# Eight loads of x moved from ahead of the last table's reads to among them

## The chip, the cores and the metric

The kernel runs on one core of a Trainium2 chip. The metric is device time in microseconds (us). Three runs of the kernel before took 4207.98, 4208.53 and 4208.92 us; the median is 4208.53 us. One more execution was profiled.

A core has five engines with a queue of their own each: TensorE (PE in the rows; PEld is its weight load), VectorE (DVE), ScalarE (ACT), GpSimd (POOL) and SyncE (SP, which here only issues DMA transfers). Every queue is worked through in order. The 16 DMA engines of the core move the data; an engine waits for data or for another engine through semaphores.

## The reference, cut to what matters

A graph layer over 12,500 atoms with 128 features and 412,500 edges, sorted by destination atom:

```
h    = maximum(layernorm(x), 0) @ W_in2f
Wij  = (softplus(f_ij @ W_f1 + b_f1) - log 2) @ W_f2 + b_f2
Wij  = Wij * rcut_ij[:, None]
x_ij = h[idx_j] * Wij                                   # 412500 x 128, a message per edge
agg  = segment_sum(x_ij, idx_i, num_segments=12500)
out  = (softplus(agg @ W_o1 + b_o1) - log 2) @ W_o2 + b_o2
return x + out
```

In the call, `idx_i` is `src` and `idx_j` is `dst`. All is float32. The last line is the part that matters here: each output row is x, plus the output bias b_o2 (into which the constant log 2 is folded), plus a product.

## The kernel before, in words

**Main loop.** The edges are worked in 806 chunks of 512. For each chunk the kernel computes the edge filter, picks the rows of h by a matmul with a comparison mask, multiplies both to 512 messages (`message`, tile `o`), and scatters them with four indirect DMAs from GpSimd's queue (`scatter`, line 873) into a table of slots in device memory. There are seven tables (`SEGS`), one after the other. While chunks run, the table that is complete is read back and summed per atom (`Collect`). The last four groups of 2048 edges go to the seventh table, `slots6`, and this one can be read only after the last scatter into it has landed.

**A table's sum.** `Collect` cuts a table into units. `load(u)` issues a read of unit u from SP into a tile `m` of seven buffers (line 919). `compare(u)` makes a 0/1 matrix `to` (five buffers) that says which of the 128 atoms of a block each slot belongs to: on VectorE in one instruction (line 932), on GpSimd in one instruction per block (line 938). `add(u)` multiplies the two on TensorE into PSUM (line 953), and `keep` adds the result to `agg` on VectorE (line 987). The seventh table has 27 units: 22 with four blocks, five with two blocks of two tiles each.

**Loads of x.** The output is made in 25 quads of four blocks, 512 atoms each (the last has two pieces, of 128 and 84 rows). Every quad needs its x rows (256 KB a quad), loaded by `x_load` from SP (line 428), and the bias added by `x_bias` (line 433). Eight early quads are loaded during the main loop, with VectorE adding the bias. The other 17, the late ones, have their tiles in buffers that the main loop has given up: `late_homes` gives eight quads in the buffers of `rel` (named `xr`), four in those of `f` (`xf`), two in those of `hg` (`xh`), three in those of `o` (`xm`). The generator `x_ahead` loads and biases them in order. For the late quads it is run in one go, after the main loop and ahead of the final table's first read, with the bias on GpSimd, where these additions stand behind the last scatters.

**The tail.** After it comes a loop over the 27 units of the final table, written out by hand: five reads are issued ahead and two comparisons made, then at each unit u the read of unit u + 5 is issued, unit u + 2 is compared (on GpSimd where u is odd and over 6, else on VectorE), unit u is summed, and the quad that is complete takes one stage further (`stages`): the first output matmul (line 443), three ScalarE functions (446, 411, 412), VectorE's line 449, the second output matmul (453), VectorE's addition to x (457), and the store from SP (460). The stages of five successive quads are in flight at once. So the order on SP is: late loads of x, five reads, and then a read and a store in turn; on GpSimd: scatters, biases, comparisons. SP's DMAs use eight completion semaphores in turn, so a DMA is not issued before the one eight places ahead of it has landed.

The loop of the tail is this:

```
for u in range(len(last.units)):
    last.load(u + 5)
    if u + 2 < len(last.units):
        last.compare(u + 2, nc.gpsimd if u > 6 and u % 2 else nc.vector)
    done = last.done
    last.done = []
    last.add(u)
    if done:
        ...
        stages(q)
        q += 1
```

Of the kernel before, what the change touches and what calls it, by code (L numbers as in the profile page):

```python
# [21 lines left out]
QT = CH // P  # L22
# [18 lines left out]
def ceil_div(a, b):  # L41
    return -(-a // b)
# [3 lines left out]
def gnn_kernel(  # L46
# [20 lines left out]
    nc = tc.nc  # L67
# [5 lines left out]
    NTILE = ceil_div(N, P)  # L73
# [47 lines left out]
    def sbuf(name, shape, dtype=F32):  # L121
        return const.tile(shape, dtype, name=name)

    def spread(t, n):
        return t[:, None, :].to_broadcast([t.shape[0], n, P])
# [21 lines left out]
    bf2, bo2 = (sbuf(n, [P, P]) for n in ("bf2", "bo2"))  # L147
# [87 lines left out]
    def relative(k):  # L235
        n = parts_c[k][1]
        d0 = ln.tile([P, 1], F32, name="d0")
        nc.vector.tensor_copy(d0[:n, :], d0_i[k][:n, :])
        nc.vector.tensor_scalar(rel[:n, k, :], dc[k][:n, :], d0[:n, :], None, op0=ALU.subtract)
# [174 lines left out]
    def x_pieces(t0, n):  # L414

        n0 = t0 * P
        full = min(n, N // P - t0)
        rest = N - n0 - full * P if full < n else 0
        pieces = []
        if full:  # L420
            pieces.append((P, slice(0, full), slice(n0, n0 + full * P)))
        if rest:
            pieces.append((rest, slice(full, n), slice(n0 + full * P, N)))
        return pieces

    def x_load(xo, pieces):
        for p, cs, rows in pieces:
            nc.sync.dma_start(xo[:p, cs, :], x[rows, :].rearrange("(c p) f -> p c f", p=p))

    def x_bias(xo, pieces, engine=nc.vector, b=bo2):  # L430
        for p, cs, rows in pieces:
            xi = xo[:p, cs, :]
            engine.tensor_add(xi, xi, spread(b[:p, :], xi.shape[1]))
# [111 lines left out]
    with tc.tile_pool(name="edge", bufs=2) as edge, tc.tile_pool(  # L545
# [491 lines left out]
        def group(j):  # L1037
            if j not in groups and j < NG:
                groups[j] = Group(j)
# [110 lines left out]
        t0, i = 8, 0  # L1150
        while i < len(segs):
# [5 lines left out]
            t0, i = due[j], j + 1  # L1157
# [20 lines left out]
        i, k = 0, todo[0][0]  # L1178
# [12 lines left out]
        def x_ahead(homes, engine, b):  # L1191

            pending = []
            for q, xo in homes:
                n = min(QT, NTILE - q * QT)
                pieces = x_pieces(q * QT, n)
                x_load(xo, pieces)
                xs[q] = xo
                pending.append((xo, pieces))
                yield  # L1200
                yield
                if len(pending) > 2:
                    x_bias(*pending.pop(0), engine, b)
            for w in pending:
                yield
                x_bias(*w, engine, b)

        def as_quad(t):
            return t.rearrange("p (c f) -> p c f", f=P)

        xs = {}
        NX = 8

        def early_homes():
            for q in range(NX):
                if q < 6:
                    yield q, ln.tile([P, QT, P], F32, name="xo", tag=("xb", "xT", "left")[q // 2],
                                     bufs=2)
                else:
                    t = ln.tile([P, QT, 3, P], BF16, name="xo", tag="hb", bufs=2)  # L1220
                    yield q, as_quad(t.rearrange("p c k f -> p (c k f)")[:, :2 * CH].bitcast(F32))

        def late_homes():
            for q in range(NX, NX + 12, 2):
                if q < NX + 8:
                    t = edge.tile([P, NCHUNK, CH], BF16, name="xr", tag="rel", bufs=4)
                    t = t.rearrange("p c e -> p (c e)").bitcast(F32)
                else:
                    t = edge.tile([P, NB, CH], F32, name="xf", tag="f")
                    t = t.rearrange("p b e -> p (b e)")  # L1230
                for i in range(2):
                    yield q + i, as_quad(t[:, i * CH:(i + 1) * CH])
            for q in range(NX + 12, NX + 14):
                yield q, quad.tile([P, QT, P], F32, name="xh", tag="hg")
            for q in range(NX + 14, NQ):
                t = quad.tile([P, QT, RW], F32, name="xm", tag="o", bufs=BACK)
                yield q, t[:, :, :P]
# [34 lines left out]
        with tc.manual_schedule():  # L1272
            constants()
            nc.scalar.activation(count_ps, places, AF.Copy)
            h = [make_h(q, psum) for q in range(2)]
            next(h[0])
            next(h[0])
            relative(0)
            shift(0)
            group(0)  # L1280
            early[1] = load_x(1)
            next(h[0])
            groups[0].edges()
            next(h[0])
            part("hidden", 0, hidden)
            groups[0].blocks(0)
            made["blocks"] = 0
            next(h[0])
            groups[0].half_log(0)
            next(h[0])  # L1290
            part("rows", 3, rows)
            biases(psum)
            bs[0] = groups[0].bias(0)
            groups[0].half_log(1)
            made["log"] = 0
            ready = ranks(0)
            next(ready)
            groups[0].starts()
            groups[0].half_end(0)
            part("window", 0, window)  # L1300
            vs[0] = groups[0].value(0, bs.pop(0))
            next(ready, None)
            made["rank"] = 0
            groups[0].half_end(1)
            made["end"] = 0
            group(1)
            aside = side()
            x_early = x_ahead(early_homes(), nc.vector, bo2_ps)
            x_late = x_ahead(late_homes(), nc.gpsimd, bo2)
            for k in range(-3, max(NCH, max(units) + 1)):  # L1310
                for seg, d in zeros.get(k, ()):
                    seg.clears.append(nc.sync.dma_start(*d).ins.name)
                now = units.get(k, ())
                for c, u in now:
                    if u == 0:
                        for i in range(AHEAD):
                            c.load(i)
                if k == NCH:
                    kept["rest"] = True
                step(k, now)  # L1320

                if k >= 0:
                    for m in h:
                        next(m, None)
                if k > NEXT - 3:
                    next(aside, None)
                if k >= XK:
                    next(x_early, None)
            summed[0].add(summed[1])
            for c in owed:  # L1330
                c.keep()
            owed.clear()
            worst = state.tile([1, 1], F32, name="worst")
            nc.vector.tensor_reduce(worst, bad, axis=mybir.AxisListType.X, op=ALU.max)
            nc.vector.tensor_copy(flag, worst)
            for _ in x_early:
                pass
            for _ in x_late:
                pass


            last = collects[-1]
            z = psum.tile([P, 2, CH], F32, name="z_out", tag="z")
            outs = []
            for q in range(NQ):
                n = min(QT, NTILE - q * QT)
                sT = kept["agg"][:, q * QT:q * QT + n, :].rearrange("p c f -> p (c f)")
                outs.append(finish(q * QT, n, sT, quad, psum, z[:, q % 2, :], xs[q]))

            def stages(q):  # L1350
                for d in (1, 2, 3, 4, 5):
                    if 0 <= q - d < NQ:
                        next(outs[q - d], None)

            for u in range(5):
                last.load(u)
            last.compare(0)
            last.compare(1)
            q = 0
            for u in range(len(last.units)):  # L1360
                last.load(u + 5)
                if u + 2 < len(last.units):
                    last.compare(u + 2, nc.gpsimd if u > 6 and u % 2 else nc.vector)
                done = last.done
# [3 lines that stand above are left out]
                    now, last.done = last.done, done  # L1368
                    last.keep()
                    last.done = now  # L1370
                    stages(q)
                    q += 1
            last.keep()
            owed.clear()
            for q in range(q, NQ + 5):
                stages(q)
# [56 lines left out]
```

## Time and profile before

| | us |
|---|---|
| median of three runs | 4208.53 |
| lowest, highest | 4207.98, 4208.92 |
| profiled execution | 4207.59 |
| its span, first to last instruction | 4205.9 |
| TensorE busy | 3305.9 (79%) |
| VectorE busy | 3134.5 (75%) |
| ScalarE busy | 2774.6 (66%) |
| GpSimd busy | 3137.6 (75%) |
| last scatter on GpSimd begins | 4108.09 |
| first read of the final table issued | 4119.62 |
| its comparison begins | 4123.84 |
| last addition to x on VectorE begins | 4198.90 |

Shares of busy time are means over the whole span, of which the stretch at the change is the last 3%. The rows that matter are those of the last 110 us. A row of a time line gives the start in us from the start of the span, the duration, the engine (SPq is SP's queue), the line, the operation with its tiles, how many instructions are merged in the row, and in brackets how long the engine idled before and what ended it. A float32 matmul is counted as two instructions, so one unit of four blocks shows as x8. A DMA share over 1 means that transfers overlapped on an engine.

### The profile page before, as it was taken

What the parts mean: (1) busy time and instruction counts of PE and PEld (TensorE: products, weight loads), DVE (VectorE), ACT (ScalarE), POOL (GpSimd) and SP (SyncE); (2) the same over time, 40 slices, a digit from 0 to 9 for tenths busy, and PEclk for the clock granted to TensorE, in tenths of its full rate; (3) what the DMA queues carried; (4) which work ended last, traced back from release to release, by engine and by line L of the source; (5) the groups of instructions that cost most, each with busy time, mean ns of one, the idle gap of its engine ahead of it and who ended that gap; (6) DMA issues with size and microseconds to landing.
All of it is one profiled execution on the core that took longest, in us unless ns stands there. A gap on an engine that the chain in (4) does not pass through costs nothing. (4 is left out here: it accounts for less than half of the span.)

```text
span 4205.9 us, 68388 instructions
## 1 busy us (share of the span) xinstructions
PE 3305.9 (79%) x21594; PEld 2564.3 (61%) x21594; DVE 3134.5 (75%) x7192; ACT 2774.6 (66%) x5494; POOL 3137.6 (75%) x3298
## 2 busy tenths in 40 slices
PE   6777667676676666678888888988888888888887
PEld 4555445444444444457776776767777767667786
DVE  7887666666555555668877887888888888888986
ACT  6887676667666666666666666766666666666624
POOL 5777777777777777777777777777777777777774
PEclk8877776667766667679999998999999999999999
DMA  5776655655444354467778777778777977787776
GB/s 173 215 231 210 193 171 178 188 158 177 142 127 132 110 169 152 139 198 235 230 227 278 226 220 214 229 227 278 232 229 205 297 230 209 235 243 213 218 231 192
DMA packets 494767, 858.10 MB, mean 204 GB/s; under 512 B 141018, under 2 KB 276558, under 8 KB 494398
## 3 DMA queue, kind: packets, MB, share of 16 engines
q1 hardware_dynamic: 390798, 640.38, 52.1%
q0 software_dynamic: 103168, 213.15, 15.0%
q8 instruction: 174, 2.85, 0.3%
q14 instruction: 195, 1.60, 0.1%
q10 hardware_dynamic: 432, 0.13, 0.0%
HBM read 457.62 MB, written 395.69 MB: 203 GB/s over the span
## 5 line engine op out<-in xcount | busy, mean ns | idle before, releaser
L873 POOL DMA_INDIRECT slots<-o,slot x3224 | 3093.3, 959 | 1011.8 <-issue 720.4
L856 ACT ACTIVATE hg<-picked,rcut 128x128 f32<-128x128 f32 x3224 | 909.6, 364 | 409.5 <-PE picked L846 396.2
L834 PEld LDWEIGHTS v<-wf,r 128*128 128x128 f32 x6448 | 997.4, 233 | 252.4 <-issue 128.1
L834 PE MATMUL v<-wf,r 128*128 128x128 f32 x6448 | 1075.4, 321 | 24.2 <-ACT v L826 11.7
L953 PEld LDWEIGHTS acc<-to,m 128*128 128x128 f32 x5660 | 723.4, 205 | 213.4 <-DVE agg L987 87.6
L826 ACT ACTIVATE v<-bf 128x512 f32<-128x512 f32 x806 | 484.8, 601 | 535.2 <-DVE o L864 516.0
L710 PE MATMUL z<-f,wf 20*128 20x512 f32 x1612 | 564.5, 783 | 346.2 <-DVE r L742 343.9
L953 PE MATMUL acc<-to,m 128*128 128x128 f32 x5660 | 768.1, 293 | 71.0 <-DVE agg L987 51.1
L863 DVE COPY o<-place 128x4 f32<-128x4 f32 x806 | 151.8, 188 | 678.7 <-DMA slots<-o,slot 677.6
L932 DVE TENSOR_TENSOR to<-numbers,m 128x640 f32<-128x640 f32 (+3 forms) x793 | 629.7, 824 | 29.4 <-DMA m<-slots 19.7
L846 PE MATMUL picked<-near,at 126*128 126x128 bf16 x3224 | 363.7, 243 | 329.2 <-DVE o L864 322.8
L864 DVE TENSOR_TENSOR o<-v,hg 128x512 f32<-128x512 f32 x806 | 552.3, 685 | 80.3 <-PE v L834 75.1
L742 DVE SCALAR_TENSOR_TENSOR r<-z,nbf,a 128x1024 f32<-128x1024 f32 x402 | 512.8, 1276 | 81.3 <-ACT a L722 80.6
L846 PEld LDWEIGHTS <-at 126*128 126x128 bf16 x3224 | 290.5, 111 | 380.4 <-issue 310.7
L747 DVE TENSOR_TENSOR inb<-numbers,blk 128x392 f16<-128x392 f32 x806 | 446.1, 554 | 96.0 <-PE numbers L953 95.7
L719 ACT ACTIVATE a<-z,bf 128x1024 f32<-128x1024 f32 x402 | 442.4, 1101 | 113.8 <-PE z L710 113.5
L722 ACT ACTIVATE a<-a,half 128x1024 f32<-128x1024 f32 x402 | 461.6, 1148 | 13.1
L710 PEld LDWEIGHTS z<-f,wf 20*128 20x128 f32 x1612 | 142.3, 215 | 522.1 <-DVE r L742 493.2
L771 DVE TENSOR_REDUCE top<-free 128x4 f32<-128x392 f32 x806 | 446.1, 553 | 13.0 <-PE free L766 12.5
L720 ACT ACTIVATE a<-a 128x1024 f32<-128x1024 f32 x402 | 424.9, 1057 | 12.7
L953 PEld LDWEIGHTS numbers<-to,m 128*128 128x128 f32 x2492 | 326.7, 211 | 156.3 <-DVE to L932 145.2
L953 PE MATMUL numbers<-to,m 128*128 128x128 f32 x2492 | 354.9, 301 | 69.7 <-DVE to L932 68.8
(126 smaller groups left out, 1984.8 us busy)
## 6 DMA issues: line engine op xcount, KB each, us to landing
m<-slots SPq DMA_DIRECT2D x307, 387.0 KB
rel<-rel_d SPq DMA_DIRECT2D x202, 504.0 KB
m<-slots SPq DMA_DIRECT2D x278, 322.5 KB
f<-in_f_t SPq DMA_DIRECT2D x101, 512.0 KB
slots<-o,slot POOLq DMA_INDIRECT x3224
m<-slots SPq DMA_DIRECT2D x193, 258.0 KB
slots<-zero SPq DMA_DIRECT2D x96, 387.0 KB
slots<-zero SPq DMA_DIRECT2D x58, 516.0 KB
```

The source lines that it names most:

```text
L710: mm = nc.tensor.matmul(z[:, k, :], wf1[rows, :], self.f[rows, :], start=True, stop=True)
L722: nc.scalar.activation(a, a, AF.Ln, bias=half, scale=0.5)
L742: nc.vector.scalar_tensor_tensor(r, z, nbf1, a, op0=ALU.max, op1=ALU.add)
L747: nc.vector.tensor_tensor(inb, count_ps[:, None, :NBLK].to_broadcast([P, QT, NBLK]), self.blk[:, c * QT:(c + 1) * QT, None].to_broadcast([ ...
L826: nc.scalar.activation(v, spread(bf12, QT), AF.Copy)
L834: mm = nc.tensor.matmul(v[:, i, :], r[:, i * P:(i + 1) * P], wf2, start=False, stop=True, skip_group_check=True)
L846: mm = nc.tensor.matmul(ps[:, i, :], at[:, i * P:(i + 1) * P], near, start=i == 0, stop=i == QT - 1, skip_group_check=True)
L856: nc.scalar.activation(hg[:, i, :], ps[:, i, :], AF.Copy, scale=self.rcut[:, j:j + 1])
L864: nc.vector.tensor_mul(o[:, :, :P], v, hg)
L873: put = nc.gpsimd.indirect_dma_start(out=views[j % VIEWS], out_offset=bass.IndirectOffsetOnAxis(ap=self.slot[:, j:j + 1], axis=0), in_=o[: ...
L932: nc.vector.tensor_tensor(to[:, :n, :], count_ps[:, None, :].to_broadcast([P, n, P]), m[:, :n, P:].to_broadcast([P, n, P]), op=ALU.is_equal)
L953: nc.tensor.matmul(self.acc[b // few][:, i, :], m[:, j, :P], to[:, j, :], start=t == 0, stop=t == self.seg.tiles(b) - 1)
```

## The change

The 17 late quads are no longer loaded and biased in one go. `NOW` = 9 of them are loaded there, and their bias is added on GpSimd as before. The other eight (three of `xf`, two of `xh`, three of `xm`) are loaded within the loop of the tail: behind the read that is issued at u = 1, 3, ... 15 stands one load of x on SP's queue. Their biases are added on GpSimd at u = 4, 6, ... 18, so that each is in GpSimd's queue three units after its load, and from u = 8 on between the comparisons that GpSimd makes at odd u. The homes of all late quads are taken at once, before the first load.

```diff
-        NX = 8
+        NX, NOW = 8, 9
...
             x_early = x_ahead(early_homes(), nc.vector, bo2_ps)
-            x_late = x_ahead(late_homes(), nc.gpsimd, bo2)
...
             for _ in x_early:
                 pass
-            for _ in x_late:
-                pass
+            late = []
+            for q, xo in late_homes():
+                xs[q] = xo
+                late.append((xo, x_pieces(q * QT, min(QT, NTILE - q * QT))))
+            for w in late[:NOW]:
+                x_load(*w)
+            for w in late[:NOW]:
+                x_bias(*w, nc.gpsimd, bo2)
...
             for u in range(len(last.units)):
                 last.load(u + 5)
+                i = NOW + u // 2
+                if u % 2 and i < len(late):
+                    x_load(*late[i])
+                if not u % 2 and NOW <= i - 2 < len(late):
+                    x_bias(*late[i - 2], nc.gpsimd, bo2)
                 if u + 2 < len(last.units):
                     last.compare(u + 2, nc.gpsimd if u > 6 and u % 2 else nc.vector)
```

Every quad is still loaded once, biased once on the same engine and stored once. On TensorE, VectorE and ScalarE the instructions and their order are unchanged. On SP, the eight moved loads (nine instructions) pass behind reads 6, 8, 10 and so on of the final table; on GpSimd the eight biases pass behind comparisons.

## The prediction

> **What bounds the kernel now.** The change touches only what comes after the last scatter of messages, so I read that stretch and nothing before it. First the table of engine time by stretch, for core 0. Its columns are the stretch, its length, busy time of the five engines with their instruction counts, the granted TensorE clock, the busy share of the 16 DMA engines and GB/s.
>
> ```profile
> span 4205.9 us, 68388 instructions
> 4095.00:4110.00 15.00, 13.98 (x120) 13.44 (x119) 12.82 (x19) 0.00 (x0) 11.62 (x13) 1.00 1.06 339
> 4110.00:4119.60 9.60, 0.70 (x7) 0.51 (x5) 0.75 (x4) 0.00 (x0) 9.60 (x9) 0.73 1.14 296
> 4119.60:4126.00 6.40, 1.37 (x6) 1.40 (x7) 1.73 (x3) 0.00 (x0) 6.40 (x6) 0.50 1.13 287
> 4126.00:4135.00 9.00, 8.24 (x47) 6.54 (x46) 5.96 (x10) 4.22 (x7) 5.35 (x9) 0.89 0.79 190
> 4135.00:4140.00 5.00, 5.00 (x35) 4.04 (x34) 3.78 (x6) 3.83 (x6) 0.99 (x3) 1.00 0.03 8
> 4140.00:4180.00 40.00, 40.00 (x271) 32.97 (x270) 33.49 (x54) 30.59 (x45) 17.49 (x31) 1.00 0.73 198
> ```
>
> TensorE is nearly idle from 4110 to about 4124 while the DMA engines are full (shares of 1.14 and 1.13). From 4140 to 4180 it is busy in all 40.00 us, and the DMA engines have room (0.73). So the end has two regimes: a hole in which transfers set the pace, then a tail that TensorE bounds. The waits of VectorE and TensorE in this stretch say what the hole waits for (total, times, longest):
>
> ```profile
> DVE to L932 <- DMA m<-slots: 13.1, 4, 12.4
> PE acc L953 <- DVE to L932: 13.9, 1, 13.9
> ```
>
> The first read of the final table (m, line 919) must land, a comparison (line 932) follows, then the first sum (line 953). What stands ahead of that read is in the SP queue's own rows (start, duration, operation, count):
>
> ```profile
> 4091.09 9.71 SPq L919 DMA_DIRECT2D m<-slots  x11
> 4100.85 9.33 SPq L428 DMA_DIRECT2D xr<-in_x  x8
> 4110.22 4.22 SPq L428 DMA_DIRECT2D xf<-in_x  x4
> 4114.53 1.65 SPq L428 DMA_DIRECT2D xh<-in_x  x2
> 4116.23 3.02 SPq L428 DMA_DIRECT2D xm<-in_x  x4
> 4119.62 13.60 SPq L919 DMA_DIRECT2D m<-slots  x12
> 4139.53 0.38 SPq L460 DMA_DIRECT2D out<-xo  x1
> 4140.01 0.46 SPq L919 DMA_DIRECT2D m<-slots  x1
> 4142.69 0.46 SPq L919 DMA_DIRECT2D m<-slots  x1
> ```
>
> Eighteen pieces of x (17 quads, the last in two pieces) go out from 4100.85, and read 0 of the final table is issued only at 4119.62. In the hole SP spends about 1 us on a load, against 0.38 to 0.46 us at 4139 and 4142: the full DMA queue pushes back. The rows of VectorE, TensorE and GpSimd at both rims of the hole, from their time lines:
>
> ```profile
> 4110.74 0.42 DVE L987 TENSOR_TENSOR agg<-agg,acc 128x256 f32<-128x256 f32 x1 [0.65 <-PE acc L953]
> 4123.84 0.69 DVE L932 TENSOR_TENSOR to<-numbers,m 128x512 f32<-128x512 f32 x1 [12.40 <-DMA m<-slots]
> 4106.41 4.29 PE L953 MATMUL acc<-to,m 128*128 128x128 f32 x36 [0.23 <-DVE to L932]
> 4124.63 4.54 PE L953 MATMUL acc<-to,m 128*128 128x128 f32 x24 [13.93 <-DVE to L932]
> 4156.98 1.11 PE L953 MATMUL acc<-to,m 128*128 128x128 f32 x8
> 4184.63 0.68 DVE L457 TENSOR_TENSOR xf<-xf,v_out 128x512 f32<-128x512 f32 x1
> 4108.09 0.95 POOL L873 DMA_INDIRECT slots<-o,slot  x1 [0.30 <-issue]
> 4109.06 9.79 POOL L433 TENSOR_TENSOR xr<-xr,bo 128x512 f32<-128x512 f32 x8
> 4126.15 3.13 POOL L433 TENSOR_TENSOR xm<-xm,bo 128x512 f32<-128x512 f32 x4
> 4145.94 2.33 POOL L938 TENSOR_SCALAR to<-places,m 128x128 f32<-128x128 f32 x4 [4.33 <-DMA m<-slots]
> ```
>
> Read 0 takes 4123.84 - 4119.62 = 4.22 us from issue to its comparison. TensorE starts 0.79 us later, after 13.93 us of idling.
>
> **The change: eight x loads leave the hole.** Before read 0 nine loads remain: eight of xr and one of xf. The next slot of SP is where the second xf was issued, and reads 0 to 6 may go from there. They need the scatters into the final table to have landed. From 4111.2 to 4123.8 the DMA page gives the first row below. The second is the scatter queue from 4113 to 4114, its last entry: from 4114 on no such row is listed. Then the issues of x from 4111.2 to 4123.8, which are exactly the loads that move, and of the table's reads.
>
> ```profile
> 4111.21 3.23 SPq L428 DMA_DIRECT2D xf<-in_x  x3
> DMA packets 7279, 3.65 MB, mean 289 GB/s; under 512 B 258, under 2 KB 7267, under 8 KB 7279
> q0 software_dynamic: 1, 0.00, 0.1%
> xf<-in_x SPq DMA_DIRECT2D x3, 256.0 KB
> xh<-in_x SPq DMA_DIRECT2D x2, 256.0 KB
> xm<-in_x SPq DMA_DIRECT2D x2, 256.0 KB
> xm<-in_x SPq DMA_DIRECT2D x1, 64.0 KB
> xm<-in_x SPq DMA_DIRECT2D x1, 42.0 KB
> m<-slots SPq DMA_DIRECT2D x7, 258.0 KB
> ```
>
> The moved bytes are 7 x 256 + 64 + 42 = 1898 KB, or 1.944 MB; at 289 GB/s that is 6.73 us. In packets of 512 B they are 3796; 7279 packets in 12.6 us are 578 per us, so 6.57 us. I take the middle, 6.65 us. This holds if the DMA engines never run dry between the ninth x load and read 0. The ninth is issued at 4110.22; with the same 4.22 us it lands near 4114.4. Read 0 can be issued when the last scatter is down, which I take as 4113.1 from the row for 4113 to 4114, so it still finds a queue. Counted from that issue instead: 4113.1 + 4.22 = 4117.3, a gain of 6.5 us. The two counts agree, and I keep 6.65: comparison 0 near 4117.2, TensorE near 4118.0.
>
> **What bounds this term.** Upper end: SP's slot alone moves from 4119.62 to 4111.21, 8.41 us, if the scatter is down by then and the latency stays. If read 0 instead finds an empty queue, the nearest row is the read issued at 4142.69 whose comparison starts at 4145.94: 3.25 us, hence 4116.35 and a gain of 7.5 us. Lower end: the scatter's end is bounded by its queue row only to the microsecond before 4114, and the rate of 289 could be 198 GB/s (the tail's row) for reads of the table; with read 0's own 258 KB that costs 0.4 us more, plus 0.9 us for the scatter: gain 5.3 us. I take 6.65 as nearest to the rows of this very stretch.
>
> [...]
>
> **The clock.** The profile's rows, microsecond by microsecond, show when it falls and returns:
>
> ```profile
> 4114.00:4115.00 1.00, 0.00 (x0) 0.00 (x0) 0.00 (x0) 0.00 (x0) 1.00 (x1) 0.69 1.14 285
> 4127.00:4128.00 1.00, 1.00 (x7) 1.00 (x7) 1.00 (x3) 0.00 (x0) 1.00 (x2) 0.50 0.70 149
> 4128.00:4129.00 1.00, 1.00 (x10) 1.00 (x10) 1.00 (x3) 0.00 (x0) 1.00 (x3) 0.98 0.86 223
> ```
>
> It falls inside 4114 to 4115, about 3.7 us after TensorE's last sum (4110.70), and is full again at 4128, 3.4 us after the restart. With a restart at 4118.0 the hole is still 7.3 us, so TensorE starts cold as now: cost and gain zero. Were it warm, the first 24 matmuls would take 3 x 1.11 = 3.33 us instead of 4.54: 1.2 us more gain. Were it cold for twice those 3.4 us at half the clock, at most 1.7 us more is lost.
>
> [...]
>
> **The loads in their new places.** One x load follows reads 6, 8, 10 and so on up to the end of the eight, on SP. Each costs SP 0.38 to 0.46 us where the queue is not full; SP has two such issues per tail step of 4142.69 - 4140.01 = 2.68 us, and waits the rest. Nothing else queues behind them but reads and stores. A read is early: read 13 lands at 4145.94, GpSimd's comparison of it ends at 4148.27, and its sum starts at 4156.98, 8.7 us later. VectorE's reads have the same lead, five reads ahead. DMA traffic: two steps (5.36 us) carry two reads (516 KB), two stores (512 KB) and one x load (256 KB), 1.315 MB, which needs 245 GB/s against 289 to 339 seen when full. Cost zero, hidden by those 8.7 us.
>
> **The additions in their new places.** GpSimd adds nine biases from 4109.06, 1.22 us each (9.79 / 8), to 4120.1, waiting for the ninth load perhaps; then eight, each between comparisons. Per 5.36 us it has 2.33 + 1.22 = 3.55 us of work. Behind a bias waits a comparison, and behind that the sum with 8.7 us to spare; a bias delays it by 1.22 us plus any wait for its x. The first of these, the second xf, is loaded behind read 6 and biased before 4126; its use is the row at 4184.63. VectorE is not slowed by GpSimd's additions: the comparison at 4123.84 took 0.69 us beside them. Cost zero.
>
> **Sum.** -6.65 us on the profiled execution: span 4205.9 to 4199.3, all of the tail shifted. That execution took 4207.59 us, 1.7 outside the span and 0.94 below the median of the runs, 4208.53. So 4208.53 - 6.65 = 4201.9, or -0.16%. A measurement of this kernel tells about 0.2%, 8.4 us, from no change; the forecast lies inside.
>
> **Rivals.**
> The queue is drained. Read 0 lands early, from the 3.25 us row up to SP's slot: 7.5 to 8.41 us gained, 4201.0 to 4200.1, and up to 1.2 us more, 4198.9, if the clock's fall comes later than the 3.7 us of the row and misses the shorter hole. For it: the last scatter frees read 0 two microseconds after the last of the nine is issued. Against: a DMA share of 1.14 all through, and 3.65 MB moved in a stretch whose own issues up to read 0 are 2.2 MB, so over a megabyte was queued before or belonged to the next reads.
>
> The wait returns partly in the tail. Reads 7 to 11 share the ramp with three x loads, or GpSimd's first comparison slips behind biases. From 4126 to 4135 the DMA share is 0.79; three loads of 0.9 us each there cost at most 2.7 us, and another 1.2 us for a bias: gain 2.7 us, 4205.8. Against: 0.03 share in the 5 us after it.
>
> Slower: DMA becomes the tail's bound. Place: the eight pairs of steps with an x load. It decides below 245 GB/s. At the tail's present 198 GB/s, which I read as a demand and not as a limit, a pair needs 6.64 us, 1.28 late; over eight pairs 10.2 us, less the lead of 8.7, still a gain of 5.1. To end slower by 0.2%, reads must lose 6.65 + 8.4 + 8.7 = 23.8 us, 3.0 us a pair, or 157 GB/s: 4217.0. Nothing full ran so slowly here.
>
> The change does not act: if the scatters landed only near 4119, read 0 would stay, 4208.5. The queue row for 4113 to 4114 is against it.
>
> **How the numbers follow.** Forecast 0.58; drained queue 0.24, most of it with the warm start or the full slot and so past 8.4 us; partial return or no effect 0.12; slower 0.06. Faster by over 0.2%: 0.20, from the drained queue and the forecast's edge. Within: 0.74. Slower: 0.06. The range runs from 4199.6, inside the drained case, to 4206.0, past the partial return; the likeliest case alone has 4200.7 to 4203.2 (5.3 to 7.85, the drained row with some clock).
>
> **What will show it.** Right: read 0 issued near 4113, with one scatter-bound wait ahead of it on SP; comparison 0 near 4117.2 and TensorE's wait near 7.3 us; steps of 2.69 us and 5.00 busy in 5.00 after that; a tail of the same length. Wrong: TensorE idling inside the tail, a DMA share near 1 there, comparisons on GpSimd that end just before their sums, or read 0 landing within 3 us of its issue.

## The result, and the profile after

The changed kernel takes 4203.81 us (median of 22 runs, 4200.22 to 4206.56); the kernel before, in 22 runs beside it, 4208.73 us (4205.96 to 4212.39). The ratio is 0.9987, with a 95% interval of 0.9981 to 0.9993: faster by 0.13%, or 4.9 us by the medians. The profiled execution took 4203.76 us, with a span of 4202.0 us.

The table of engine time by stretch, of the changed kernel, with the columns as before:

```profile
4110.00:4119.60 9.60, 3.89 (x35) 3.70 (x34) 3.50 (x7) 0.00 (x0) 7.21 (x6) 0.87 1.02 277
4119.60:4126.00 6.40, 5.25 (x27) 4.81 (x28) 5.44 (x9) 0.00 (x0) 3.83 (x4) 0.66 1.06 266
4140.00:4180.00 40.00, 40.00 (x269) 32.78 (x268) 33.48 (x54) 30.19 (x46) 22.10 (x34) 1.00 0.76 213
```

The stretch of the hole has more work in it, and the tail is still full on TensorE, 40.00 us of 40.00. The DMA share there rose only from 0.73 to 0.76, since half of the x loads fall ahead of 4140. The time lines of SP, GpSimd, VectorE and TensorE at the rims of the hole:

```profile
4103.31 10.26 SPq L428 DMA_DIRECT2D xr<-in_x  x8
4113.61 0.76 SPq L428 DMA_DIRECT2D xf<-in_x  x1
4114.74 5.88 SPq L919 DMA_DIRECT2D m<-slots  x7
4120.67 0.76 SPq L428 DMA_DIRECT2D xf<-in_x  x1
...
4107.80 0.96 POOL L873 DMA_INDIRECT slots<-o,slot  x1 [0.30 <-issue]
4142.17 2.33 POOL L938 TENSOR_SCALAR to<-places,m 128x128 f32<-128x128 f32 x4 [0.58 <-DVE agg L987]
...
4119.95 0.69 DVE L932 TENSOR_TENSOR to<-numbers,m 128x512 f32<-128x512 f32 x1 [5.32 <-DMA m<-slots]
4193.47 1.67 DVE L457 TENSOR_TENSOR xm<-xm,v_out 128x512 f32<-128x512 f32 x4
...
4109.61 4.29 PE L953 MATMUL acc<-to,m 128*128 128x128 f32 x36 [1.09 <-DVE to L932]
4120.74 4.46 PE L953 MATMUL acc<-to,m 128*128 128x128 f32 x24 [6.85 <-DVE to L932]
```

Three things are to be seen. TensorE's wait went from 13.93 to 6.85 us, 7.08 us shorter. The tail, from the start of its first sum to the start of the last row of additions to x, is 4193.47 - 4120.74 = 72.73 us. But the sixth table's sum ended at 4109.61 + 4.29 = 4113.90, where it ended at 4110.70 in the profile before. So 3.2 of the 7.1 us are missing from the span, and they went missing ahead of the first changed instruction: the first load of x, which stands ahead of all that was changed, was itself issued 2.46 us later, at 4103.31 instead of 4100.85.

### The profile page after: what moved, and what is told of

Same layout as the page of the kernel before. It is cut to its first block, busy times and chain, and to the rows that moved or that the text cites. A ratio compares the mean times of both kernels' runs of the same rounds, so it can differ in the third digit from the quotient of the medians.

```text
span 4202.0 us, 68386 instructions
## 1 busy us (share of the span) xinstructions
PE 3299.9 (79%) x21594; PEld 2559.1 (61%) x21594; DVE 3134.2 (75%) x7192; ACT 2774.6 (66%) x5494; POOL 3138.5 (75%) x3298
## 5 line engine op out<-in xcount | busy, mean ns | idle before, releaser
L834 PEld LDWEIGHTS v<-wf,r 128*128 128x128 f32 x6448 | 987.0, 231 | 243.9 <-issue 135.8
L834 PE MATMUL v<-wf,r 128*128 128x128 f32 x6448 | 1064.3, 319 | 17.4 <-ACT v L826 10.5
L953 PEld LDWEIGHTS numbers<-to,m 128*128 128x128 f32 x2492 | 341.8, 219 | 154.5 <-DVE to L932 143.6
L953 PE MATMUL numbers<-to,m 128*128 128x128 f32 x2492 | 369.7, 310 | 66.4 <-DVE to L932 65.5
```

Source lines behind the costliest of these rows:

```text
L834: mm = nc.tensor.matmul(v[:, i, :], r[:, i * P:(i + 1) * P], wf2, start=False, stop=True, skip_group_check=True)
L953: nc.tensor.matmul(self.acc[b // few][:, i, :], m[:, j, :P], to[:, j, :], start=t == 0, stop=t == self.seg.tiles(b) - 1)
```

## The experiments

Four marks are read from each trace: the wait of TensorE ahead of the seventh table's first sum (the hole), the length from the start of that sum to the start of the last row of line 457 (the tail), the end of the last scatter on GpSimd, and the issue of read 0. Runs 1 to 4 were on a chip where the kernel before takes 4207.93 us (27 runs), runs 5 to 12 on one where it takes 5034 to 5075 us. There the main loop is slower, and the granted TensorE clock is 0.78 to 0.79 on average in the profiled executions, against 0.84; what causes the difference stays open. Its times spread over 20 to 40 us, so from that chip the marks carry more than the times. The kernel before was timed there but not profiled.

**1. The kernel before, again.** No edit.

> The kernel before, unchanged, profiled once more, to see how far the marks of the last 110 us move from one execution to the next. In the first profile of before the last scatter began at 4108.09 us, the sixth table's last sum ended at 4110.70, read 0 was issued at 4119.62, the first sum of the seventh table began at 4124.63 and the last addition to x at 4198.90; in the profile of the change the sixth table ended at 4113.90, 3.2 us later, though nothing ahead of it was changed. Theory 'chance': the sixth table's end moves by some 2 to 3 us between executions of one kernel, against the last scatter. Rival 'systematic': here it ends within 0.5 us of 4110.7, and the change has made it later.

Its single time was 4211.28 us. TensorE's rows at the hole:

```profile
4108.52 4.30 PE L953 MATMUL acc<-to,m 128*128 128x128 f32 x36 [0.38 <-DVE to L932]
4127.09 5.46 PE L953 MATMUL acc<-to,m 128*128 128x128 f32 x24 [14.27 <-DVE to L932]
```

The hole is 14.27 us, near the first 13.93. The sixth table ends at 4112.82, 2.1 us later than in the first profile of the same kernel. So this mark does move by about 2 us from one execution to the next, as "chance" has it, and a pair of spans from one profile each can't size a change of 7 us. The hole can: it is measured between two rows of one trace. The tail is 74.17 us here, 1.4 longer than in the first profile of the same kernel; the part on the clock comes back to this.

**2. The changed kernel, again.** No edit.

> The changed kernel, unchanged, profiled and timed once more. Theory 'queue' (what stands ahead of read 0 in the DMA queue sets the hole): TensorE's wait ahead of the seventh table's first sum is 6 to 8 us, and the time is 5 to 7 us under that of before. Rival 'systematic' (the change also delays the sixth table's end by 3 us): its last sum ends again 5 us or more after the last scatter's end, and the time is about 4 us under.

4202.34 us (11 runs), ratio 0.9989 (0.9980 to 0.9998), 5.6 us under by the medians. SP's wait for the scatters, its rows, the last scatter, one row of DMA traffic (SP's queue from 4115 to 4116), the first comparison, and TensorE's rows:

```profile
SPq L919 <- DMA slots<-o,slot: 2.2, 3, 1.0
4111.72 0.95 SPq L428 DMA_DIRECT2D xf<-in_x  x1
4115.18 4.35 SPq L919 DMA_DIRECT2D m<-slots  x7
4109.68 0.96 POOL L873 DMA_INDIRECT slots<-o,slot  x1 [0.30 <-issue]
q1 hardware_dynamic: 195, 0.09, 37.0%
4118.49 0.69 DVE L932 TENSOR_TENSOR to<-numbers,m 128x512 f32<-128x512 f32 x1 [5.72 <-DMA m<-slots]
4106.28 5.75 PE L953 MATMUL acc<-to,m 128*128 128x128 f32 x48 [1.14 <-DVE to L932]
4119.28 4.65 PE L953 MATMUL acc<-to,m 128*128 128x128 f32 x24 [7.25 <-DVE to L932]
```

The hole is 7.25 us, the sixth table ends at 4112.03. It ended only 1.4 us after the last scatter (4110.64), not 5 us or more, so "systematic" falls in its strong form: this execution has its sixth table earlier than run 1 of the kernel before. But another gate shows. SP was through with the ninth load at 4112.67 and issued read 0 only at 4115.18: it waited for the last scatter, whose instruction had ended at 4110.64, so the landing took about 4.5 us. Meanwhile the DMA engines drained: SP's queue kept them 37% busy from 4115 to 4116. In the first profile of the change read 0 followed its ninth load with no such wait. Which of the two gates binds depends on how the last scatter falls against the sixth table's reads in that execution.

**3. The eight loads in one block behind read 4.**

```diff
             for u in range(5):
                 last.load(u)
+            for w in late[NOW:]:
+                x_load(*w)
+            for w in late[NOW:]:
+                x_bias(*w, nc.gpsimd, bo2)
...
                 last.load(u + 5)
-                i = NOW + u // 2
-                if u % 2 and i < len(late):
-                    x_load(*late[i])
-                if not u % 2 and NOW <= i - 2 < len(late):
-                    x_bias(*late[i - 2], nc.gpsimd, bo2)
```

> The eight loads stand in one block right behind reads 0 to 4 of the final table, and their biases right behind the first nine, instead of one by one among the reads. Theory 'queue': what counts is that they are behind read 0; hole and time as in the changed kernel, 6 to 8 us and 5 to 7 us under before, and read 5 on is late by up to 8 x 0.9 = 7 us, which the lead of 8.7 us covers. Rival 'spreading matters': the block delays reads 5 to 12 and GpSimd's first comparison, TensorE idles 2 us or more in the ramp, and the time is 2 to 4 us worse than the changed kernel's.

4208.83 us (11 runs), ratio 1.0003 (0.9994 to 1.0012): the whole gain is gone, and I had expected most of it to stay. SP's rows, the last scatter, VectorE's comparisons of units 0 and 5, and TensorE's waits from 4108 to the end:

```profile
4118.69 2.57 SPq L919 DMA_DIRECT2D m<-slots  x5
4130.56 7.92 SPq L919 DMA_DIRECT2D m<-slots  x7
4112.68 0.96 POOL L873 DMA_INDIRECT slots<-o,slot  x1 [0.30 <-issue]
4121.40 0.69 DVE L932 TENSOR_TENSOR to<-numbers,m 128x512 f32<-128x512 f32 x1 [7.04 <-DMA m<-slots]
4134.66 0.69 DVE L932 TENSOR_TENSOR to<-numbers,m 128x512 f32<-128x512 f32 x1 [7.58 <-DMA m<-slots]
PE acc L953 <- DVE to L932: 8.6, 1, 8.6
PE acc L953 <- DVE agg L987: 5.2, 1, 5.2
```

The hole is 8.57 us, the tail 81.26 us, 8.5 longer. Read 5 is issued at 4130.56, after the block. Its comparison waits 7.58 us at the head of VectorE's queue, and an addition to agg stands behind it, for which TensorE's next sum waits 5.2 us. The rest of the 8.5 us fits the granted clock, which fell a second time: its mean was 0.85 from 4130 to 4137 and 0.83 from 4140 to 4145, from which I estimate 0.50 from 4135 to 4141.7. No run shows the two parts on their own. So "behind read 0" is not enough. The lead of 8.7 us that I read off unit 13 belongs to the settled tail; unit 5 has no such lead. Spreading the loads is a needed part of the change. SP also waited for the last scatter here, until 4118.69; by then the DMA engines moved only 24 GB/s (4118 to 4119), and read 0 took 2.71 us to its comparison.

**4. The eight loads and their biases left out.** The last eight quads are added to the tiles of the eight before them, so those output rows are not the reference's.

```diff
+            for q in range(NX + NOW, NQ):
+                xs[q] = xs[q - 8]
             for w in late[:NOW]:
                 x_load(*w)
...
-                i = NOW + u // 2
-                if u % 2 and i < len(late):
-                    x_load(*late[i])
-                if not u % 2 and NOW <= i - 2 < len(late):
-                    x_bias(*late[i - 2], nc.gpsimd, bo2)
```

> The eight moved loads and their biases are left out altogether: the last eight quads of the output are added to the tiles of the eight quads ahead of them, so these rows are not the reference's. It prices the loads in their new places. Theory 'queue': they are hidden there, so time and tail length (74.2 us from the first sum of the seventh table to the last addition to x) are those of the changed kernel within 1 us. Rival 'the tail pays': without them the kernel is 2 us or more faster than the changed one, from reads that land sooner or a shorter tail.

4202.37 us (11 runs), ratio 0.9987 (0.9978 to 0.9996), beside 4202.34 us of run 2. TensorE:

```profile
4108.94 6.03 PE L953 MATMUL acc<-to,m 128*128 128x128 f32 x48 [0.96 <-DVE to L932]
4121.75 5.01 PE L953 MATMUL acc<-to,m 128*128 128x128 f32 x24 [6.78 <-DVE to L932]
```

The hole is 6.78 us, the tail, to the same addition, 73.29 us (72.73 with the loads). Without the loads nothing is gained: in their new places they cost nothing that can be measured. "The tail pays" falls. This trace, too, has its sixth table late, at 4114.97.

**5 to 7. Thirteen, seven and five loads ahead of read 0.** The edit is one constant and the places of the rest; each bias stays three units behind its load. With five ahead:

```diff
-        NX, NOW = 8, 9
+        NX, NOW = 8, 5
+        AT = (0, 1, 2, 3, 4, 5, 7, 9, 11, 13, 15, 17)
...
-                i = NOW + u // 2
-                if u % 2 and i < len(late):
-                    x_load(*late[i])
-                if not u % 2 and NOW <= i - 2 < len(late):
-                    x_bias(*late[i - 2], nc.gpsimd, bo2)
+                if u in AT:
+                    x_load(*late[NOW + AT.index(u)])
+                if u - 3 in AT:
+                    x_bias(*late[NOW + AT.index(u - 3)], nc.gpsimd, bo2)
```

> Thirteen late loads stay ahead of read 0, four are among the reads (behind those issued at u = 1, 3, 5, 7; biases three units later). Theory 'queue, then scatter' (read 0 goes when the loads ahead of it are through AND the last scatter has landed, 4.4 to 5 us after GpSimd's instruction): four more loads make the queue the gate in every execution; TensorE's hole is 10 to 11 us, SP does not wait for a scatter, and the time is 2 to 3.5 us under before. Rival 'only the scatter' (the queue does not matter once half is moved): hole and time as in the changed kernel, 7 us and 5 us under.

> Seven late loads ahead of read 0, ten among the reads: behind those issued at u = 1 to 5, 7, 9, 11, 13, 15, biases three units later. Theory 'queue, then scatter': SP waits for the scatter in most executions; hole 5.5 to 7 us, time 0 to 1.5 us under the changed kernel's, 5 to 7 under before. Rival 'queue alone': two loads of 0.9 us fewer, hole 5.2 us, 1.8 us under the changed kernel's. Rival 'the ramp pays', after the block behind read 4 cost 8 us: TensorE waits for a comparison in the ramp, and the time is 1 us or more over the changed kernel's.

> Five late loads ahead of read 0, twelve among the reads: behind those issued at u = 0 to 5, 7, 9, 11, 13, 15, 17, biases three units later. Theory 'queue, then scatter': SP waits 1.5 to 4 us for the scatter in every execution and the DMA engines run dry meanwhile; hole 5 to 7 us, the time within 1.5 us of that with seven ahead. Rival 'queue alone': hole 3.5 us, 3.6 us under the changed kernel's, so about 9 under before. Rival 'the ramp pays': TensorE waits in the ramp, 1 us or more over the changed kernel's.

First sums of the seventh table, with thirteen ahead:

```profile
4951.59 5.34 PE L953 MATMUL acc<-to,m 128*128 128x128 f32 x24 [10.25 <-DVE to L932]
```

with seven:

```profile
4945.35 4.42 PE L953 MATMUL acc<-to,m 128*128 128x128 f32 x24 [4.77 <-DVE to L932]
```

and with five:

```profile
4933.37 4.68 PE L953 MATMUL acc<-to,m 128*128 128x128 f32 x24 [3.05 <-DVE to L932]
```

The times, beside 5034.54 us of before: 5033.07 us (ratio 0.9999, 0.9987 to 1.0012), 5028.45 us (0.9983, 0.9970 to 0.9996), 5024.56 us (0.9989, 0.9977 to 1.0001). The medians fall with the holes, but only the second ratio stands clear of 1, and the ratios don't put five below seven. With thirteen ahead the 2 to 3.5 us that I had expected are not shown. On this chip the scatters are no gate at all: in the trace with five ahead the last one begins at 4866.7, 60 us ahead of read 0, and SP waits for none. So what I expected of the scatter here did not come about, and "queue alone" describes this chip: it expected 5.2 and 3.5 us with seven and five ahead. The ramp, the first steps of the tail, paid nothing in this trace either: the tail with five ahead is 72.96 us.

**8, 9 and 12. All seventeen behind the reads**, one behind each read issued at u = 0 to 16. The rest of the edit is that of run 7.

```diff
-        NX, NOW = 8, 9
+        NX, NOW = 8, 0
+        AT = tuple(range(17))
```

> All 17 late loads among the reads, one behind each read issued at u = 0 to 16, biases three units later. It doubles the transfers of the tail: a step of 2.69 us then carries a read, a store and an x load, 770 KB, which needs 293 GB/s, as much as the full queue gave in the hole (285 to 310). Theory 'queue, then scatter': nothing stands ahead of read 0 but the scatter, hole 4.5 to 6.5 us, and the tail is 0 to 4 us longer than the 72.8 us of before, so the time is 2 to 7 us under before. Rival 'DMA becomes the tail's bound', the slower rival of the prediction at its strongest: the tail is 5 us or more longer, with TensorE waiting in it, and the gain is gone.

> All 17 late loads among the reads, once more. In its first run the before kernel took 5034 us, the last scatter began some 60 us ahead of read 0, and neither the scatter nor the tail cost anything: hole 1.44 us, time 0.27% under. Where before takes about 4208 us the last scatter lands beside the end of the sixth table. Theory 'queue, then scatter': there SP waits for it 3 us or more, hole 4.5 to 7 us, the DMA engines run dry in the hole, and the time is 4 to 9 us under before; where before is at 5034 us again, 11 to 17 us under. Rival 'queue alone': 12 us or more under in both.

> All 17 late loads among the reads, a third time, in the hope of a chip on which before takes about 4208 us. Theory 'queue, then scatter': there SP waits for the last scatter, the hole is 4.5 to 7 us and the time 4 to 9 us under before; if before is above 5000 us again, SP does not wait, the hole is 1 to 2 us and the time 8 to 17 us under.

5020.60 us beside 5034.54 (ratio 0.9973, 0.9963 to 0.9984), 5066.99 beside 5075.30 (0.9975, 0.9962 to 0.9988) and 5023.55 beside 5034.39 (0.9977, 0.9965 to 0.9988): 8 to 14 us under in three sessions; run 9, at 8.3, is under the 11 to 17 us expected for this chip, which its interval still holds. From run 8: VectorE's first comparisons and TensorE's first sums of the seventh table, TensorE's longest wait from 4932 on, the last additions, and the tail's table row:

```profile
4932.67 2.46 DVE L932 TENSOR_TENSOR to<-numbers,m 128x512 f32<-128x512 f32 x4
4933.44 2.02 PE L953 MATMUL acc<-to,m 128*128 128x128 f32 x16 [1.44 <-issue]
PE acc L953 <- issue: 1.4, 1, 1.4
5005.21 1.67 DVE L457 TENSOR_TENSOR xm<-xm,v_out 128x512 f32<-128x512 f32 x4
4950.00:4990.00 40.00, 40.00 (x271) 33.05 (x270) 32.90 (x52) 30.18 (x46) 30.16 (x43) 1.00 0.92 256
```

The hole is gone, where 4.5 to 6.5 us were expected: 1.44 us are left in all three traces, and the comparison ahead of them no longer waits for a DMA. The granted clock stays at 1.00 (run 8, 4918.60 to 4951.60): two units take 2.02 us, where the first three took 4.46 us in the first profile of the change. The DMA share in the tail is 0.92, and TensorE is still busy 40.00 us in 40.00. The tail is 71.77 us (71.78 and 71.79 in runs 9 and 12). So the tail carries all seventeen loads, and the slower rival falls even with twice the added traffic. On the first chip, where the scatter can be the gate, this version was not run; what it gives there stays open. Where it ran, it beats the kernel before; against the changed kernel there is one session (runs 9 and 11), 8.6 us less by the medians.

**10 and 11. Five ahead again, and the changed kernel, beside run 9.** No further edit.

> Five late loads ahead of read 0, once more, beside the one with none. Theory 'queue, then scatter': where the scatter is the gate (before at 4208 us), five loads ahead fill the time until it lands and cost nothing, so this is within 1.5 us of none ahead; where it is not (5034 us), it is 1.5 to 4 us slower than none ahead, with a hole of 3 us. Rival 'queue alone': slower than none ahead by 1.5 to 4 us in both.

> The changed kernel beside these two. Theory 'queue, then scatter': where before is at 4208 us, hole 6.5 to 8.5 us, 4 to 6.5 us under before, 0 to 3 us slower than five ahead; where it is at 5034 us the queue is the only gate, hole 6.5 to 7 us, 6 to 8 us under before, and 3 to 5 us slower than five ahead.

5065.51 us (ratio 0.9979, 0.9965 to 0.9993) and 5075.61 us (1.0004, 0.9989 to 1.0019), where before takes 5075.30. TensorE's first sums with five ahead, and in the changed kernel:

```profile
4975.06 2.44 PE L953 MATMUL acc<-to,m 128*128 128x128 f32 x16 [2.71 <-DVE to L932]
4984.59 5.20 PE L953 MATMUL acc<-to,m 128*128 128x128 f32 x24 [6.62 <-DVE to L932]
```

The changed kernel's hole is what was expected, 6.62 us; its time is not. The interval reaches from 5.6 us under before to 9.6 us over, so the 6 to 8 us under that I had expected lie just outside it, and on this chip no gain of the change itself is shown. Why stays open; a hole of before was not traced there. With five ahead the hole is 2.71 us, and its tail 74.86 us, 1.9 longer than in run 7, with slow matmuls for longer: the 8 of a unit still took 1.74 us when they began 6.8 us after the first sum (4981.89), where in run 7 they took 1.05 us 5.4 us after it (4938.74). Five and none ahead can't be told apart by time (5065.51 and 5066.99), though 1.5 to 4 us were expected.

On the second chip the holes are 10.25, 6.62, 4.77 and 3.05 us with 13, 9, 7 and 5 loads ahead: 0.91, 0.93 and 0.86 us a load; run 10, the second trace with five, lies 0.34 us below run 7. Counted from the issue of the first load of x to the first sum, which leaves out when the sixth table ends, they are 19.21, 15.11, 13.09 and 12.18 us (11.19 in run 10): 0.88 to 1.00 us a load. This line is the strongest evidence of the study. Bytes ahead of read 0 set the hole: 256 KB in 0.90 us are 291 GB/s, and the full queue of the hole before moved 289.

## Why the prediction was right

**The term that carries it.** 6.65 us for eight loads, 7.41 full ones by their bytes, is 0.90 us each; the slope over runs 5, 11, 6 and 7 is (10.25 - 3.05) / 8 = 0.90. The hole shrank by 7.08 us between the first two profiles, and by 7.05 between the means of two each ((13.93 + 14.27) / 2 against (6.85 + 7.25) / 2). Mechanism and size of the hole hold. The hole also holds a part that the change did not make, since it begins where the sixth table happens to end. Counted from the issue of the first load of x, the first sum came after 23.78 and 23.97 us in the two traces of before, and after 17.43, 17.58 and 17.22 us in those of runs with nine ahead (first profile, runs 2 and 4): 6.46 us less by the means, still nearer to the 6.65.

**The sum.** Forecast -6.65 us, measured -4.9 and -5.6 by the medians, with intervals of 2.9 to 8.0 and 0.8 to 8.4 us. The forecast lies inside both, so an error of the sum isn't shown. The 4203.81 us themselves lie in the stated range, but 0.6 us above the band of the likeliest case alone, which ended at 4203.2. If the sum has an error, of 1 to 2 us, it isn't in the hole or the tail, but more likely in when the sixth table ends: 4110.70 and 4112.82 in two traces of before, 4112.03 to 4114.97 in four with nine loads ahead. These overlap, and no run here settles whether the change moves it. The forecast marks of read 0 and its comparison, 4113 and 4117.2, were missed in the first profile (4114.74 and 4119.95), mostly because all of it began later: counted from the first load of x the comparison was forecast at 16.35 us, and came at 16.64.

**The last scatter.** Taken as landed at 4113.1, 4.1 us after its instruction, with one wait of SP for it. In the first profile of the change there was none, in the second 2.2 us. The landing took about 4.5 us in run 2 and 5.0 in run 3 (4112.68 + 0.96 to 4118.69). So this term was a little small; that the scatter could become the gate was right in some executions. It cost little: counted from the first load of x the first sum came after 17.58 and 17.72 us in runs 2 and 3, at most 0.5 us more than in the two traces without that wait.

**The latency of read 0.** Taken as 4.22 us. It was 5.21 us in the first profile (4114.74 to 4119.95) with the queue full (DMA shares of 0.90 to 1.17), and 3.3 us in run 2 (4115.18 to 4118.49, VectorE's comparison) with the queue drained (37% from 4115 to 4116). One latency does not describe both. What holds is the count in bytes. That the prediction's second count, scatter down plus 4.22 us, came to nearly the same gain is luck in its parts: read 0 was issued 0.8 us earlier than that count has it, counted from the first load of x, and took 1.0 us longer. In run 3 it was 2.71 us (4118.69 to 4121.40), after the DMA engines had run nearly dry (24 GB/s from 4118 to 4119). So the prediction's sign of being wrong, a read 0 that lands within 3 us of its issue, did appear there, without a larger gain: SP's wait for the scatter had taken the time that the read saved.

**The clock.** Cost and gain zero, and the 24 first matmuls took 4.46 us after the shorter hole against 4.54 before. The granted clock was at 0.50 after both (4127 to 4128 before, 4122 to 4123 after). After every hole from 3.05 to 14.27 us the first 24 took 4.42 to 5.61 us, where 24 just ahead of the hole took 3.08 us in run 7; from these lengths I estimate that the clock was low after each of them. Over the 33 us around the restart its mean was 0.90 in runs 2 and 11, with holes of 7.25 and 6.62 us, and 0.95 in run 7, with 3.05 us. After the hole of 2.71 us (run 10) the first 16 matmuls took 2.44 us and the next 8 2.08 us, against 2.02 and 1.16 us after the holes of 1.44 us; by these lengths the clock fell there only 1.4 us after the restart, an estimate. After the holes of 1.44 us no row is slow, and in run 8 the clock stayed at 1.00. The holes of 3.05 and 2.71 us are shorter than the 3.7 us after which the clock fell in the first profile of before, and the matmuls behind them were slow all the same. The prediction had taken the low clock to last as long as before, 3.4 us from the restart. It was back 3.2 us after the restart in the first profile of the change (0.51 from 4123 to 4124, then 1.00). From the lengths of the rows I estimate 6.2 us in run 1, where the two matmuls of line 443 at 4132.35 still took 1.49 us against 1.12 at 4134.61, and a low clock for 6.8 us in run 10. The tails go with it: 72.73, 74.17 and 74.86 us, against 71.8 in the three traces with holes of 1.44 us. So a start at the full clock looks worth about 1 us, near the 1.2 us of the prediction; those three traces also load x elsewhere, so this is not shown on its own.

**The loads and additions in their new places.** Cost zero: the tail is 72.73 us against 4197.43 - 4124.63 = 72.80 before, and run 4 shows no gain without them. GpSimd's third comparison began at 4142.17, and nothing waited for it. Right result, but one reason was too broad: the lead of 8.7 us that I gave to all reads holds for unit 13 and those like it, while run 3 shows unit 5 with next to none. The change stays clear of that because its first load stands behind read 6.

**The rivals.** The drained queue came about in runs 2 and 3, and in run 2 it brought no larger gain, since the queue drained only while read 0 waited. Partial return in the tail: not seen. DMA as the tail's bound: not at 0.76 of the DMA engines, nor at 0.92 with all seventeen loads. No effect: excluded by the hole.

## What to carry to other kernels

Here what counted of a queue was what stood ahead of the first transfer on the critical chain. Count its bytes at the rate that the profile shows when the DMA engines are full; here that gave 0.90 us a load, and four experiments lay on the line, with a fifth 0.34 us off it. Transfers that are needed late go among the later ones where an engine bounds the stage, but spread out: in one block they starved the first steps, whose lead was smaller than the 8.7 us of the settled stage: in run 3 unit 5's comparison waited 7.58 us, and the tail grew by 8.5 us. And size such a change by the wait between two rows of one trace, since spans of single executions differed by more than half of it.

## What the runs showed that I had not expected

The kernel before took 4208 us on one chip and 5034 to 5075 us on another. The changed kernel had nearly the same tail on both (73.48 us in run 11 against 72.73) and a scatter instruction of 962 ns against 958 (medians). On the slower chip the last scatter began about 60 us ahead of the final table's first read (4916.7 against 4978.40 in run 11), so one of the two gates was missing there. So a change at the joint of two streams can have another bound on another chip. SP took about 1.1 to 1.3 us for each load of x while the DMA engines were full (8.91 to 10.26 us for eight, on the first chip), against 0.46 to 0.55 us for most of those in the tail.
